# Layer 0 of a four-layer graph network: the keys divided at 1024, masked scores negated, the row minimum carried from part to part

## The chip, the core and the metric

The kernel runs on one core of a Trainium2 chip, in float32 throughout. The core's engines work from queues of their own and wait for one another through semaphores. The names of the profile are used below: PE is TensorE (PEld its weight loads), DVE is VectorE, ACT is ScalarE, POOL is GpSimd, SP is SyncE, which here only issues DMAs. The metric is the device time of one launch in microseconds (us), lower is better.

## The reference, cut to what matters

Four graph layers are applied to 2708 nodes with 512 features; the adjacency matrix `adj` is 2708 x 2708, of zeros and ones, with a full diagonal. Each layer's result is added to its input and layer-normed. The change touches layer 0 alone, masked attention with 8 heads of 64:

```python
def _L0_gnn_ref(node_matrix, adjacency_matrix, Wks, Wqs, Wvs, Wo):
    ...
    adj = jnp.maximum(adjacency_matrix, jnp.eye(n, dtype=adjacency_matrix.dtype))
    keys = jnp.einsum('nj,hjk->hnk', node_matrix, Wks)
    queries = jnp.einsum('nj,hjk->hnk', node_matrix, Wqs)
    values = jnp.einsum('nj,hjk->hnk', node_matrix, Wvs)
    atts = jnp.einsum('hqk,hmk->hqm', queries, keys) / key_dim ** 0.5
    atts = atts - 1e+16 * (1.0 - adj)[None, :, :]
    atts = jax.nn.softmax(atts, axis=-1)
    return jnp.einsum('hqm,hmk,hko->qo', atts, values, Wo)
...
x = _layernorm(x + _L0_gnn_ref(x, adj, ...), axis=-1)
```

Layers 1 and 3 are normalized graph convolutions and layer 2 is a second attention; nothing of them is changed.

## The kernel before, in words

The 2708 nodes are 22 chunks of 128 (`NC = 22`, the last one has 20 rows). Layer 0 first projects keys (`KT`), values (`V`) and queries, then works through 85 items. An item is one chunk of 128 queries and one pair of heads (`Pair(c, p)`, four pairs a chunk); the last chunk, of 20 queries, does its four pairs in one item (`Last`), which goes first.

For each item the 2708 keys are taken in two parts, `k = 0` and `k = 1`, which begin at the chunks in `bounds` (0 and 11: 1408 and 1300 keys). The steps of an item:

- `scores(k, part)`: each part of the keys in three slices (`PARTS = 3`, of 469, 470, 433 or 434 keys). For each slice PE makes the products of the two heads (line 419) into two PSUM banks; DVE adds the mask (0 or -1e16) and keeps the slice's row maximum (line 441, one instruction for each head). A `READ_ACCUMULATOR` instruction behind each of them writes that maximum into a column of `mx`. That is 12 slices by head in an item.
- `maxima()`: DVE takes the largest of the six columns of each head, negated (`nm`, line 454).
- `weights(k)`: ACT computes exp(s - maximum) in place, one instruction for each head, with the row's sum (line 460).
- The weights must be turned, keys on the partitions, before they can be multiplied with the values. The first 8 chunks of each part (`DEALT = 8`) are turned by DVE in 32 x 32 blocks (`blocks(k)`, line 466, into a buffer `d`) and then dealt over the partitions by four DMAs of 256 KB (`deal(k)`, line 475, from `d` into a buffer `e`). The other chunks (`turned`: 8, 9, 10 and 19, 20, 21) are turned on PE (`turn()`, line 492) and copied out of PSUM by ACT (lines 495 to 498).
- `values()`: PE multiplies the turned weights with V (line 511) into the PSUM bank `av`; ACT copies the result (line 529) and POOL's queue stores it (line 530).

The order on PE, DVE and ACT is the program's own (`manual_schedule`). Three items are in work at a time. In iteration i `new` is item i, `cur` item i-1 and `late` item i-2, and each engine does:

- PE: `new.scores`, `late.values`, `cur.turn`
- DVE: `new.scores` (12), `maxima`, `cur.blocks(1)` (both heads in one instruction of 128 x 2048), `new.blocks(0)` (an instruction of 128 x 1024 for each head), and in every fourth iteration `loops` (line 209) between the scores
- ACT: `cur.weights(1)`, a row sum (line 195) and the mask (line 215) of the next chunk in three of four iterations, `new.weights(0)`, the copy of `av`, three copies out of `turn`
- SP: the loads for the next chunk, `cur.deal(1)`, `new.deal(0)`

The buffers: scores `s0` and `s1` (one for each part of the keys, two buffers each), `d` two buffers, `e` three, the PSUM banks of scores and turned blocks (`ps_s`) seven in turn, `av` one. A buffer is written again only when all who used it are done.

Of the kernel before, what the change touches and what calls it, by code (L numbers as in the profile page):

```python
# [8 lines left out]
F32 = mybir.dt.float32  # L9
AF = mybir.ActivationFunctionType  # L10
ALU = mybir.AluOpType
AX = mybir.AxisListType
# [3 lines left out]
P = 128  # L16
BLK = 512
LN_EPS = 1e-5
LOW = -3.0e38
# [3 lines left out]
def kernel(  # L23
# [22 lines left out]
    nc = tc.nc  # L46
# [4 lines left out]
    NC = (N + P - 1) // P  # L51
# [6 lines left out]
    def cols(b):  # L58
        return b * BLK, min(BLK, N - b * BLK)
# [6 lines left out]
    small = ctx.enter_context(tc.tile_pool(name="small", bufs=4))  # L66
# [51 lines left out]
    ends = [0, 8, 16, NC]  # L118
    KD4 = P // 32
    HALVES = 2  # L120
    PARTS = 3
    DEALT = 8
    bounds = [0, NC // 2, NC]

    def dealt(c):
        return any(a <= c < a + DEALT for a in bounds[:-1])
# [19 lines left out]
    with ExitStack() as l0:  # L146
# [19 lines left out]
        def load_chunk(c, k):  # L166

            r0, q = rows(c)
            if k == 0:
                a = adjp.tile([P, N], F32, tag="adj", name=f"adj{c}")  # L170
                qt = io.tile([P, NP, P], F32, tag="qt", name=f"qt{c}")
                loaded[c] = (a, qt)
            a, qt = loaded[c]
            if k < NW:
                n0, w = batch(k)
                if c < LAST:
                    nc.sync.dma_start(a[:q, n0 : n0 + w], adj[r0 : r0 + q, n0 : n0 + w])
                    return

                for g in range(0, P, 32):  # L180
                    nc.sync.dma_start(a[g : g + 32, n0 : n0 + w], adj[N - 32 :, n0 : n0 + w])
            else:
                if c == LAST:
                    nc.sync.dma_start(qt[:, :, :FILL], qtd[c - 1][:, :, P - FILL :])
                nc.sync.dma_start(qt[:, :, FILL:32] if c == LAST else qt, qtd[c])

        def row_sums(c, k):

            r0, q = rows(c)
            a = loaded[c][0]  # L190
            n0, w = batch(k)
            dst = dgp[:, c, k : k + 1]
            if c == LAST:
                q, dst = 32, dgz[:, k : k + 1]
            nc.scalar.activation(a[:q, n0 : n0 + w], a[:q, n0 : n0 + w], AF.Copy, accum_out=dst[:q])
            if c == LAST and k == NW - 1:
                nc.sync.dma_start(dgp[:LR, c, :], dgz[FILL:32, :])

        def loops(c, k):

            r0, q = rows(c)
# [15 lines left out]
        with tc.tile_pool(name="kvw", bufs=1) as kvw, tc.tile_pool(name="xTb", bufs=2) as xtp, tc.tile_pool(  # L217
            name="ps_0", bufs=8, space=PSUM
# [63 lines left out]
            for b in order:  # L282
                n0, w = cols(b)
# [100 lines left out]
        ps_a = l0.enter_context(tc.tile_pool(name="ps_a", bufs=1, space=PSUM, reuse_waits="tile"))  # L384
        ps_s = l0.enter_context(tc.tile_pool(name="ps_s", bufs=7, space=PSUM, reuse_waits="tile"))
        sp = l0.enter_context(tc.tile_pool(name="sp", bufs=2, reuse_waits="tile"))
        dp = l0.enter_context(tc.tile_pool(name="dp", bufs=2, reuse_waits="tile"))
        ep = l0.enter_context(tc.tile_pool(name="ep", bufs=3, reuse_waits="tile"))
        ptp = l0.enter_context(tc.tile_pool(name="ptp", bufs=1, reuse_waits="tile"))

        def half(k):

            n0 = bounds[k] * P
            return n0, min(bounds[k + 1] * P, N) - n0

        def bank(shape, name):
            return ps_s.tile(shape, F32, tag="s", name=name)
# [3 lines left out]
        class Pair:  # L401


            def __init__(self, c, p):
                self.c, self.p = c, p
                self.s = []
                self.mx = small.tile([P, 2, HALVES * PARTS], F32, tag="mx", name=f"mx{c}_{p}")
                self.D = {}
                self.E = {}
                self.pts = {}  # L410
                self.done = 0
                self.av = None
# [15 lines left out]
            def scores(self, k, part):  # L428

                c, p = self.c, self.p  # L430
                a = loaded[c][0]
                n0, w = half(k)
                if part == 0:
                    self.s.append(sp.tile([P, 2, w], F32, tag=f"s{k}", name=f"s{c}_{p}_{k}"))
                s = self.s[k]
                h0, h1 = (w * i // PARTS for i in (part, part + 1))
                col = k * PARTS + part
                pss = [bank([P, BLK], f"pss{c}_{p}_{col}_{j}") for j in range(2)]
                self.products(pss, n0 + h0, h1 - h0)
                for j in range(2):  # L440
                    nc.vector.tensor_tensor_reduce(  # L441
                        out=s[:, j, h0:h1],
                        in0=pss[j][:, : h1 - h0],
                        in1=a[:, n0 + h0 : n0 + h1],
                        scale=1.0,
                        scalar=LOW,
                        op0=ALU.add,
                        op1=ALU.max,
                        accum_out=self.mx[:, j, col : col + 1],
                    )  # L450

            def maxima(self):
                self.nm = small.tile([P, 2], F32, tag="nm", name=f"nm{self.c}_{self.p}")
                nc.vector.tensor_reduce(self.nm, self.mx, AX.X, ALU.max, negate=True)  # L454

            def weights(self, k):

                for j in range(2):
                    s = self.s[k][:, j, :]
                    nc.scalar.activation(s, s, AF.Exp, bias=self.nm[:, j : j + 1], accum_out=self.sums(j, k))  # L460

            def blocks(self, k, heads=slice(0, 2)):

                if k not in self.D:
                    self.D[k] = dp.tile([P, KD4, 2, DEALT, 32], F32, tag="d", name=f"d{self.c}_{self.p}_{k}")
                nc.vector.transpose(  # L466
                    self.D[k].rearrange("p i j m x -> p j m i x")[:, heads],
                    self.s[k][:, heads, : DEALT * P].rearrange("p j (m i x) -> p j m i x", i=KD4, x=32),
                )

            def deal(self, k):
# [139 lines left out]
        with tc.manual_schedule(  # L611
            engines={mybir.EngineType.PE, mybir.EngineType.DVE, mybir.EngineType.Activation}
        ):
            for i in range(len(items) + 2):
                new = None
                more = i < len(items) and items[i][0] < LAST - 1
                prep = more and items[i][1] > 0
                if cur is not None:
                    cur.weights(1)
                if i < len(items):  # L620
                    c, p = items[i]
                    if more:
                        load_chunk(c + 1, p)
                    new = (Pair if c < LAST else Last)(c, p)
                    for part in range(PARTS):
                        new.scores(0, part)
                    if prep:
                        row_sums(c + 1, p - 1)
                    new.scores(1, 0)
                    if prep:  # L630
                        loops(c + 1, p - 1)
                        mask(c + 1, p - 1)
                    for part in range(1, PARTS):
                        new.scores(1, part)
                    new.maxima()
                    new.weights(0)
                if i in (HALF0 * NP + 2, len(items)):
                    sums = heads_sums(i == len(items))
                if late is not None:
                    late.values()  # L640
                if cur is not None:
                    cur.blocks(1)
                    cur.deal(1)
                if new is not None:
                    for j in range(2):
                        new.blocks(0, slice(j, j + 1))
                    new.deal(0)
                if cur is not None:
                    cur.turn()
                if i in (HALF0 * NP + 3, len(items) + 1):  # L650
                    heads_rows(*sums)
                if i == NP:
                    last_sums()
                late, cur = cur, new
# [83 lines left out]
    with tc.tile_pool(name="wo", bufs=1, reuse_waits="tile") as wop:  # L738
        wo_sb = wop.tile([P, KC, D], F32, tag="wo", name="wo_sb")
        load_rows(wo_sb, wo)  # L740
        for c in range(NC):
# [5 lines left out]
            heads = rz_d if c == LAST else rs_d[c >= HALF0][c % HALF0]  # L747
            heads = heads.rearrange("j p q -> j (p q)")
# [129 lines left out]
    if True:  # L878
# [115 lines left out]
        for b in range(NB):  # L994
            for m, _ in enumerate(graph1(b)):
# [90 lines left out]
    if True:  # L1086
# [84 lines left out]
    with tc.tile_pool(name="zp", bufs=2) as zp:  # L1171
# [87 lines left out]
        w = cols(TAIL)[1]  # L1259
# [129 lines left out]
```

## Time and profile before

| what | before |
|---|---|
| median of 3 runs (lowest to highest) | 2587.2 us (2579.19 to 2588.0) |
| the profiled execution | 2581.24 us, of which the span from the first to the last instruction is 2579.4 us |
| mean granted TensorE clock | 0.993 |
| busy in the span: PE, DVE, ACT, POOL | 2508.7, 1962.2, 1154.0, 315.7 us |
| layer 0's 85 items (span 211 to 1226 us): PE, DVE, ACT busy, DMA share | 1003.8, 969.8, 745.5 us of 1015 us, 0.77 |
| before them (0 to 211 us): DVE busy | 117.2 us |
| after them (1226 to 2579 us): DVE busy | 875.2 us |

In the timeline a line gives the start and the length of an instruction in us, the engine, the line of the kernel, the operation, output and inputs with their shapes (partitions x elements), and in brackets how long the engine stood idle before it and what ended that. Consecutive instructions of one line are merged (x3). Instructions of DVE overlap a little: the next one can start some 0.08 us before the length of the last one is over, so the distance from start to start is what an instruction costs in a queue that is never empty.

### The profile page before, as it was taken

To read this page: it belongs to the slowest core of one execution; us is meant where nothing else is said; L and a number is where in the kernel's file an instruction comes from. 1 tells how busy PE (TensorE), PEld (TensorE's weight loads), DVE (VectorE), ACT (ScalarE), POOL (GpSimd) and SP (SyncE) were. 2 spreads that over 40 slices of the span, in tenths; PEclk is the share of its full clock that TensorE was granted. 3 is DMA by queue.
4 is the path that set the end of the run, shared out by engine and by line. 5 is a ranking of instruction groups with operands and counts; after the bars stand their busy time and mean duration, and the time that the engine had idled before them with its cause. 6 is when DMAs were issued, how large, how long until landed. Compare 5 with 4: busy or idle time off the path is not lost. (4 is left out here: it accounts for less than half of the span.)

```text
span 2579.4 us, 42415 instructions
## 1 busy us (share of the span) xinstructions
PE 2508.7 (97%) x15551; PEld 1558.2 (60%) x15551; DVE 1962.2 (76%) x4541; ACT 1154.0 (45%) x2070; POOL 315.7 (12%) x322
## 2 busy tenths in 40 slices
PE   9998999999999999999899999899999999999997
PEld 4886777777777777777456444444444465444465
DVE  3668999999999999999574777988776874543544
ACT  3104778777777777776011001565665640000000
POOL 2110000000000000000210000243332430000000
PEclk9999999999999999999999999999999999999999
DMA  5114787877877777877853444354433213644633
GB/s 167 62 50 138 218 226 211 240 213 220 230 210 219 218 211 215 225 204 186 236 169 94 126 121 142 118 158 138 125 109 116 64 31 114 184 141 143 178 103 105
DMA packets 221498, 411.43 MB, mean 160 GB/s; under 512 B 28765, under 2 KB 48911, under 8 KB 221292
## 3 DMA queue, kind: packets, MB, share of 16 engines
q1 hardware_dynamic: 215052, 392.00, 53.4%
q0 software_dynamic: 6240, 16.73, 1.9%
q8 instruction: 123, 2.02, 0.3%
q14 instruction: 83, 0.68, 0.1%
HBM read 213.55 MB, written 16.72 MB: 89 GB/s over the span
## 5 line engine op out<-in xcount | busy, mean ns | idle before, releaser
L460 ACT ACTIVATE s<-s,nm 128x1408 f32<-128x1408 f32 (+1 forms) x340 | 481.1, 1416 | 244.3 <-DVE nm L454 244.3
L441 DVE CUSTOM_DVE_ANT_0 s<-pss,adj 128x469 f32<-128x469 f32 (+2 forms) x1020 | 565.8, 622 | 8.2 <-PE pss L419 7.0
L419 PE MATMUL pss<-KT,qt 64*128 64x469 f32 (+2 forms) x2016 | 463.7, 561 | 7.2 <-DVE mx L441 4.6
L466 DVE STREAM_TRANSPOSE d<-s 128x1024 f32<-128x1024 f32 (+1 forms) x255 | 393.7, 1580 | 31.6 <-DMA e<-d 16.1
L419 PEld LDWEIGHTS pss<-KT,qt 64*128 64x128 f32 x2016 | 230.1, 187 | 200.3 <-issue 110.8
L811 PE MATMUL acc<-pt,x 128*128 128x512 f32 (+1 forms) x880 | 333.4, 537 | 12.2 <-ACT pt L864 9.7
L511 PE MATMUL av<-e,V 128*64 128x128 f32 x5376 | 309.6, 273 | 4.7 <-DMA e<-d 4.7
L511 PEld LDWEIGHTS av<-e,V 128*64 128x64 f32 x5376 | 297.8, 137 | 5.1 <-issue 5.1
L811 PEld LDWEIGHTS acc<-pt,x 128*128 128x128 f32 x880 | 157.2, 191 | 188.1 <-issue 162.2
L917 PE MATMUL acc<-at,h 128*128 128x512 f32 (+1 forms) x504 | 196.8, 543 | 0.0
L875 POOL TENSOR_TENSOR cs<-cs,pt 128x512 f32<-128x512 f32 (+2 forms) x110 | 157.3, 1430 | 202.7 <-ACT pt L864 200.4
L862 DVE TENSOR_TENSOR pt<-pt,at 128x512 f32<-128x512 f32 (+2 forms) x132 | 107.3, 820 | 75.6 <-ACT pt L861 75.4
L530 POOL DMA_DIRECT2D otd<-ot x84 | 45.2, 538 | 941.7 <-ACT ot L529 921.4
L94 ACT ACTIVATE ln_t<-lnve 128x1 f32<-128x1 f32 x88 | 17.7, 201 | 313.2 <-DVE lnve L108 313.1
L1251 ACT ACTIVATE z<-pz,rdeg 128x512 f32<-128x512 f32 (+1 forms) x22 | 15.1, 688 | 310.9 <-PE pz L823 310.9
L917 PEld LDWEIGHTS acc<-at,h 128*128 128x128 f32 x504 | 90.2, 190 | 101.4 <-issue 99.2
L492 PE MATMUL pst<-ident,s 128*128 128x128 f32 x1020 | 130.0, 277 | 0.0
L864 ACT ACTIVATE pt<-pt 128x512 f32<-128x512 f32 (+2 forms) x132 | 76.1, 579 | 110.0 <-DVE pt L863 109.8
L511 PEld LDWEIGHTS av<-pt,V 128*64 128x64 f32 x1680 | 90.0, 136 | 52.3 <-issue 51.5
L928 DVE SCALAR_TENSOR_TENSOR cs<-at,rdeg,cs 128x512 f32<-128x512 f32 (+2 forms) x126 | 86.2, 684 | 43.7 <-DMA at<-in_adjT_dram 42.4
L492 PEld LDWEIGHTS pst<-ident,s 128*128 128x128 f32 x1020 | 104.2, 133 | 16.8 <-issue 15.1
L511 PE MATMUL av<-pt,V 128*64 128x128 f32 x1680 | 110.3, 278 | 0.2 <-ACT pt L498 0.2
(348 smaller groups left out, 3474.5 us busy)
## 6 DMA issues: line engine op xcount, KB each, us to landing
e<-d SPq DMA_DIRECT2D x680, 256.0 KB
at<-in_adjT_dram SPq DMA_DIRECT2D x210, 256.0 KB
a<-in_adj_dram SPq DMA_DIRECT2D x38, 677.0 KB
adj<-in_adj_dram SPq DMA_DIRECT2D x42, 512.0 KB
at_a<-in_adjT_dram SPq DMA_DIRECT2D x40, 256.0 KB
at_c<-in_adjT_dram SPq DMA_DIRECT2D x40, 256.0 KB
at_f<-in_adjT_dram SPq DMA_DIRECT2D x40, 256.0 KB
adj<-in_adj_dram SPq DMA_DIRECT2D x21, 330.0 KB
```

Of the source, the lines that this page charges most:

```text
L419: nc.tensor.matmul(pss[j][:, :w], qt[h, self.p, :], KT[h, self.p, n0 : n0 + w], start=True, stop=True)
L441: nc.vector.tensor_tensor_reduce(out=s[:, j, h0:h1], in0=pss[j][:, : h1 - h0], in1=a[:, n0 + h0 : n0 + h1], scale=1.0, scalar=LOW, op0=ALU ...
L460: nc.scalar.activation(s, s, AF.Exp, bias=self.nm[:, j : j + 1], accum_out=self.sums(j, k))
L466: nc.vector.transpose(self.D[k].rearrange("p i j m x -> p j m i x")[:, heads], self.s[k][:, heads, : DEALT * P].rearrange("p j (m i x) -> ...
L492: nc.tensor.transpose(pt[:q, t, j, :], self.s[f][:, j, o : o + q], ident)
L511: nc.tensor.matmul(self.av[j * KD : (j + 1) * KD, out], V[:, m, h * KD : (h + 1) * KD], weights[j], start=(self.done == 0), stop=(self.don ...
L811: nc.tensor.matmul(acc[k][:, :w], last[0][g : g + mr, :] if m == NC - 1 else values[:mr, k * P : (k + 1) * P], moving[g : g + mr, :w], sta ...
L862: nc.vector.tensor_tensor(pt[:mr, :w], pt[:mr, :w], at[:mr, :w], ALU.subtract)
L864: nc.scalar.activation(pt[:mr, :w], pt[:mr, :w], AF.Exp)
L875: nc.gpsimd.tensor_tensor(sums[:mr, :w], sums[:mr, :w], pt[:mr, :w], ALU.add)
L917: nc.tensor.matmul(acc[hc][:, :w], lastH[g : g + mr, :] if m == NC - 1 else H[m][:mr, hc * P : (hc + 1) * P], at[g : g + mr, :w], start=(m ...
L928: nc.vector.scalar_tensor_tensor(sums[:mr, :w], at[:mr, :w], rdeg[:mr, m : m + 1], sums[:mr, :w], ALU.mult, ALU.add)
```

## The change

The second part of the keys now begins at chunk 8 (`bounds = [0, 8, 22]`): the parts have 1024 and 1684 keys, in 2 and 4 slices (512 and 421 keys). Chunks 0 to 7 and 8 to 15 are dealt, 16 to 21 are turned on PE, all of them from the second part. The scores are stored negated (`scale=-1.0`), so that the row's extreme is a minimum; each slice starts its minimum from the column that the slice in front of it wrote (`scalar=self.mx[:, j, col - 1 : col]`, a value for each partition, read from memory; the first slice of each head has the constant `-LOW`). The last column is then the minimum of all keys, and `maxima()` is gone; exp is taken with `scale=-1.0` and that column as its bias. `s0` has one buffer instead of two, `d` three instead of two, and `new.blocks(0)` turns both heads in one instruction.

```diff
-    PARTS = 3
+    PARTS = (2, 4)
     DEALT = 8
-    bounds = [0, NC // 2, NC]
+    bounds = [0, DEALT, NC]
...
-        dp = l0.enter_context(tc.tile_pool(name="dp", bufs=2, reuse_waits="tile"))
+        dp = l0.enter_context(tc.tile_pool(name="dp", bufs=3, reuse_waits="tile"))
...
-                    self.s.append(sp.tile([P, 2, w], F32, tag=f"s{k}", name=f"s{c}_{p}_{k}"))
+                    self.s.append(sp.tile([P, 2, w], F32, tag=f"s{k}", name=f"s{c}_{p}_{k}", bufs=k + 1))
...
-                h0, h1 = (w * i // PARTS for i in (part, part + 1))
-                col = k * PARTS + part
+                h0, h1 = (w * i // PARTS[k] for i in (part, part + 1))
+                col = sum(PARTS[:k]) + part
...
                     nc.vector.tensor_tensor_reduce(
                         out=s[:, j, h0:h1],
                         in0=pss[j][:, : h1 - h0],
                         in1=a[:, n0 + h0 : n0 + h1],
-                        scale=1.0,
-                        scalar=LOW,
+                        scale=-1.0,
+                        scalar=self.mx[:, j, col - 1 : col] if col else -LOW,
                         op0=ALU.add,
-                        op1=ALU.max,
+                        op1=ALU.min,
                         accum_out=self.mx[:, j, col : col + 1],
                     )
-            def maxima(self):
-                self.nm = small.tile([P, 2], F32, tag="nm", name=f"nm{self.c}_{self.p}")
-                nc.vector.tensor_reduce(self.nm, self.mx, AX.X, ALU.max, negate=True)
...
-                    nc.scalar.activation(s, s, AF.Exp, bias=self.nm[:, j : j + 1], accum_out=self.sums(j, k))
+                    nc.scalar.activation(s, s, AF.Exp, scale=-1.0, bias=self.mx[:, j, -1:], accum_out=self.sums(j, k))
...
-            def blocks(self, k, heads=slice(0, 2)):
-                if k not in self.D:
-                    self.D[k] = dp.tile([P, KD4, 2, DEALT, 32], F32, tag="d", name=f"d{self.c}_{self.p}_{k}")
+            def blocks(self, k):
+                self.D[k] = dp.tile([P, KD4, 2, DEALT, 32], F32, tag="d", name=f"d{self.c}_{self.p}_{k}")
                 nc.vector.transpose(
-                    self.D[k].rearrange("p i j m x -> p j m i x")[:, heads],
-                    self.s[k][:, heads, : DEALT * P].rearrange("p j (m i x) -> p j m i x", i=KD4, x=32),
+                    self.D[k].rearrange("p i j m x -> p j m i x"),
+                    self.s[k][:, :, : DEALT * P].rearrange("p j (m i x) -> p j m i x", i=KD4, x=32),
                 )
...
-                    new.maxima()
                     new.weights(0)
...
-                    for j in range(2):
-                        new.blocks(0, slice(j, j + 1))
+                    new.blocks(0)
                     new.deal(0)
```

More of the change, by code (lines that the diff above doesn't have):

```diff
@@ L406, in __init__ @@
                 self.s = []
-                self.mx = small.tile([P, 2, HALVES * PARTS], F32, tag="mx", name=f"mx{c}_{p}")
+                self.mx = small.tile([P, 2, sum(PARTS)], F32, tag="mx", name=f"mx{c}_{p}")
                 self.D = {}
@@ L624 @@
                     new = (Pair if c < LAST else Last)(c, p)
-                    for part in range(PARTS):
+                    for part in range(PARTS[0]):
                         new.scores(0, part)
@@ L632 @@
                         mask(c + 1, p - 1)
-                    for part in range(1, PARTS):
+                    for part in range(1, PARTS[1]):
                         new.scores(1, part)
-                    new.maxima()
                     new.weights(0)
```

## The prediction

> **What bounds the kernel now.** The change touches only layer 0's 85 items, so I read the groups of instructions first for those lines, then one iteration in the timelines of DVE and PE, then DVE's waits over 300 to 1200 us.
>
> From the page (groups; last columns: busy us, mean ns, idle before and its releaser):
>
> ```profile
> L460 ACT ACTIVATE s<-s,nm 128x1408 f32<-128x1408 f32 (+1 forms) x340 | 481.1, 1416 | 244.3 <-DVE nm L454 244.3
> L441 DVE CUSTOM_DVE_ANT_0 s<-pss,adj 128x469 f32<-128x469 f32 (+2 forms) x1020 | 565.8, 622 | 8.2 <-PE pss L419 7.0
> L466 DVE STREAM_TRANSPOSE d<-s 128x1024 f32<-128x1024 f32 (+1 forms) x255 | 393.7, 1580 | 31.6 <-DMA e<-d 16.1
> ```
>
> ACT has 244 us to spare. DVE hardly waits before its scores, and 31.6 us before its transposes. One undisturbed iteration, DVE from `nm` to `nm`, then PE from turn to turn:
>
> ```profile
> 256.55 0.17 DVE L454 TENSOR_REDUCE nm<-mx 128x2 f32<-128x12 f32 x1
> 256.75 4.56 DVE L466 STREAM_TRANSPOSE d<-s 128x2048 f32<-128x2048 f32 x3
> 261.25 0.65 DVE L441 CUSTOM_DVE_ANT_0 s<-pss,adj 128x469 f32<-128x469 f32 x1
> ...
> 267.83 0.09 DVE L441 DVE_READ_ACCUMULATOR2_ANT mx<- 128x1 f32 x1
> 267.95 0.17 DVE L454 TENSOR_REDUCE nm<-mx 128x2 f32<-128x12 f32 x1
> ...
> 258.70 1.53 PE L492 MATMUL pst<-ident,s 128*128 128x128 f32 x12
> ...
> 260.16 5.06 PE L419 MATMUL pss<-KT,qt 64*128 64x469 f32 x24
> ...
> 265.15 1.31 PE L511 MATMUL av<-pt,V 128*64 128x128 f32 x20
> ...
> 270.10 1.53 PE L492 MATMUL pst<-ident,s 128*128 128x128 f32 x12
> ```
>
> DVE: 0.20 from `nm` to the transposes, 4.50 for three transposes, 6.58 for twelve slices, 0.12 from the last read of the accumulator to `nm`: 11.40 us, with no idle in it. PE: 1.46 turning, 4.99 scores, 4.95 values: also 11.40, dense. So both engines have the same floor. Yet from 281.26 to 1216.59 us there are 79 iterations in 935.3 us, 11.84 each. The 37 of them with no idle on DVE in front of a transpose have a mean of 11.47 (11.41 without, about 11.60 with a `loops` instruction, which takes 0.2); the other 42 have 12.17. The waits behind that:
>
> ```profile
> DVE d L466 <- DMA e<-d: 15.1, 30, 1.5
> DVE d L466 <- ACT ot L529: 5.5, 6, 1.0
> DVE d L466 <- ACT pt L498: 3.3, 2, 1.9
> ```
>
> Nothing that `blocks` reads comes from `ot` or `pt`, so those waits too are the DMA's. With two `d` buffers `blocks(0)` writes what the dealing of the last `blocks(0)` has to have left, 11.40 - 2.3 = 9.1 us later; only that transpose waits, hardly ever `blocks(1)`.
>
> **The change part by part**, on DVE, which has no slack.
>
> 1. Third `d` buffer. `blocks(0)` now takes the buffer that `blocks(1)` left a whole iteration (over 11 us) earlier, and those DMAs are issued first of the eight; `blocks(1)` waits on DMAs twice as old. Before, `blocks(1)` came 9.5 us after the `blocks(1)` whose buffer it took and did not wait, so landing within 9.5 us is shown and the waits end. Worth 42 x (12.17 - 11.47) = 29 us at most (12.17 also holds some `loops`), 26 us by the idle alone. PE's use of `e` is two iterations behind for part 0 and PE waited for no DMA in this stretch, so the DMA has nowhere new to be late.
>
> 2. `nm` gone: 0.12 + 0.20 = 0.32 us an item. The transposes read no `mx`, so the first can follow the last slice directly.
>
> 3. One transpose for both heads: the three took 4.50 start to start. The 128x1024 form takes 1.13 start to start (1.067 for its elements if one takes 1/0.96 ns, which is what 469 against 433 elements, 0.567 against 0.53 us, gives), so the 128x2048 form 4.50 - 2.26 = 2.24; two are 4.48: 0.02 saved, 0.1 if the large one's fixed part is as small as the other's. I take 0.06. It must wait for both heads' exp. A 1408-wide exp takes 1.47 start to start, a 1300-wide 1.38, so a 1024-wide one 1.15. The first head's minimum is ready one slice (0.57) before the last; exp then ends about 1.9 us after the last slice, under `blocks(1)`'s 2.24. If waits went by the whole `mx` tile it would end at some 2.5, a stall of 0.3 or 24 us over the run. ACT itself is free: `weights(1)` grows by 2 x 0.32 (1684 for 1300 keys) and `weights(0)` may come 0.8 earlier, against an idle of 244.3/85 = 2.9 us an item.
>
> 4. The carried minimum: ten of an item's twelve slices now read a scalar from memory. No slice of before does. The nearest rows, instructions of 512 elements a partition, first without such a scalar, then with one (`rc`, `rdeg`):
>
> ```profile
> 102.65 0.69 DVE L236 TENSOR_TENSOR cx<-xp 128x512 f32<-128x512 f32 x1
> 103.25 0.69 DVE L237 TENSOR_TENSOR cx<-xp 128x512 f32<-128x512 f32 x1
> ...
> 1429.44 0.29 DVE L945 TENSOR_TENSOR rc<-pcs,rdeg 128x1 f32<-128x1 f32 x3 [0.63 <-PE pcs L734]
> 1429.65 0.74 DVE L952 SCALAR_TENSOR_TENSOR y<-b_sb,rc,x 128x512 f32<-128x512 f32 x1
> 1430.31 0.75 DVE L928 SCALAR_TENSOR_TENSOR cs<-at,rdeg,cs 128x512 f32<-128x512 f32 x1
> 1430.97 0.15 DVE L945 TENSOR_TENSOR rc<-pcs,rdeg 128x1 f32<-128x1 f32 x1
> ```
>
> 0.60 start to start without, 0.66 with: 0.06 for the scalar. Bounds: 0, if the accumulator read between two slices covers the fetch, and 0.12, what `nm` lost waiting for the read just ahead of it. I take 0.06, the row nearest in kind: 10 x 0.06 = 0.60 us an item. The order of reads is harmless: a slice's scalar was written by the read two slices back, with the other head's slice between, and L952 above, which reads column 0 of `rc`, started 0.07 behind the write of column 2, so waits go by column. Negating, the constant of the first slice and exp's scale are constants in place of constants: 0. The elements (2 x 2708) and the number of slices stay, so 6.58 + 0.60.
>
> 5. One `s0` buffer: the first slice overwrites what the transpose right ahead of it reads. The nearest pair is L381 writing what the reduction L382 ahead of it read:
>
> ```profile
> 187.25 0.69 DVE L382 TENSOR_REDUCE u<-wk_sb 128x1 f32<-128x512 f32 x1
> 187.97 0.69 DVE L381 TENSOR_TENSOR wk_sb<-wk_sb 128x512 f32<-128x512 f32 x1
> ```
>
> 0.72, where independent ones take 0.60: 0.12. I take that; 0 is the other end. PE no longer reads `s0`, so nothing but DVE and ACT's finished exp stands in front of it.
>
> 6. PE: 512 and 421 keys for 469 and 433 are the same columns, matmuls and turned blocks; 0. It falls from co-bound to 0.3 us of slack, and cannot go below 11.40.
>
> **The sum.** An iteration of DVE: 6.58 + 0.60 + 4.44 + 0.12 = 11.74; `loops` in every fourth adds 0.05: 11.79, against 11.84. Over 79 iterations that is 4 us less; what was won from the DMA (29) goes back into ten slower slices (47) less `nm` and the merged transpose (30) and plus the overwritten buffer (9). From the profiled execution's 2581.2 that makes 2577; the median of the runs shown is 6 higher, which would make it 2583. I name 2579. My forecast is no change. Its own range: the overwrite at 0 gives 13 less, the scalar at 0.07 gives 8 more: 2566 to 2590.
>
> [...]
>
> **The rivals.**
>
> *The scalar is free (0.22).* Then DVE needs 11.74 - 0.60 = 11.14 and PE becomes the bound at 11.41: 79 x 0.43 = 34 us less, 2547. For it: the accumulator read already costs next to nothing beside the slice that follows. Against: every row with a scalar shows its 0.06, also back to back.
>
> *The carried column is waited for (0.16), slower.* Place: each of the ten slices on DVE, which has no slack. Price: 0.12 instead of 0.06, 0.60 more an item: 12.39, 79 x 0.55 = 43 us more, 2624. It decides from 0.07 a slice on, where the iteration passes 11.84, and is past my bound of 13 us at 0.08. For it: the read right ahead of `nm` did cost 0.12. Against: here it lies one slice back.
>
> *The third buffer does not end the waits (0.08),* because the dealing itself is behind, not the buffer: then 26/79 = 0.33 stays in each iteration, 12.12, 22 us more: 2603. For it: the DMA share is already 0.77. Against: undisturbed stretches run at 11.40 with the same DMAs, and `blocks(1)` never waits.
>
> **How the numbers follow.** No change 0.50, of which 0.10 lies lower than 0.5% (13 us, about what a measurement of this kernel can tell); the rivals 0.22, 0.16, 0.08; 0.04 is left to stalls I do not see, half of them slower ones. Faster: 0.22 + 0.10 + 0.01 = 0.33. Slower: of 0.16 some 0.14, of 0.08 all but 0.02, 0.02 of the rest and 0.02 of the forecast: 0.24. Same: 0.43. The range runs from the free scalar, 2545, to just short of the full price of the wait, 2618.
>
> **What would show it.** Step 4: slices of 512 and 421 start 0.67 and 0.57 apart (0.61 and 0.52 if free, 0.73 and 0.63 if waited for). Step 1: no idle of DVE before L466. Step 2: the first transpose starts with the last accumulator read. Step 3: none of the idle before L466 is ACT's exp. Step 5: 0.12 more from the last transpose to the first slice. Step 6: PE's iteration has gaps before L419 that end with DVE. What would make it wrong most easily is step 4, whose error counts 790 times.

## The result, and the profile after

| | before | after |
|---|---|---|
| median (lowest to highest) of 6 runs each | 2586.46 us (2578.86 to 2588.0) | 2603.6 us (2598.36 to 2608.85) |
| ratio to before, 95% interval | 1 | 1.0075 [1.0057, 1.0093] |
| profiled execution, its span | 2581.24, 2579.4 us | 2603.68, 2601.9 us |
| mean granted TensorE clock | 0.993 | 0.989 |

The changed kernel is 0.75% slower: the means of the six runs are 19 us apart, the spans of the two profiled executions, which are compared below, 22.5 us. The time lies inside the predicted range, but the forecast, no change, was wrong: a gain of 4 us was expected.

From the page of the changed kernel, the groups that answer to those of before (the slices are now two groups, with and without `mx` as a scalar):

```profile
L456 ACT ACTIVATE s<-s,mx 128x1024 f32<-128x1024 f32 (+1 forms) x340 | 480.9, 1415 | 224.5 <-DVE mx L441 224.4
L441 DVE CUSTOM_DVE_ANT_0 s<-pss,adj,mx 128x421 f32<-128x421 f32 (+1 forms) x850 | 514.6, 671 | 0.0
...
L461 DVE STREAM_TRANSPOSE d<-s 128x2048 f32<-128x2048 f32 x170 | 382.4, 2286 | 1.9 <-ACT s L456 1.9
...
L441 DVE CUSTOM_DVE_ANT_0 s<-pss,adj 128x512 f32<-128x512 f32 x170 | 110.7, 689 | 31.1 <-PE pss L419 18.3
```

The transposes stood idle 31.6 us before and 1.9 us now, none of it for a DMA. The slices are busy 625.3 us instead of 565.8. Of these idle times only one has grown, that in front of the slices: 31.1 us against 8.2, all before the first slice of a head. Of these, 16.4 belong to the third iteration below; most of the rest are 0.14 us in nearly every item. One steady iteration of DVE, from transpose to transpose:

```profile
606.73 0.08 DVE L441 DVE_READ_ACCUMULATOR2_ANT mx<- 128x1 f32 x1
606.73 4.50 DVE L461 STREAM_TRANSPOSE d<-s 128x2048 f32<-128x2048 f32 x2
611.37 0.69 DVE L441 CUSTOM_DVE_ANT_0 s<-pss,adj 128x512 f32<-128x512 f32 x1
...
612.60 0.74 DVE L441 CUSTOM_DVE_ANT_0 s<-pss,adj,mx 128x512 f32<-128x512 f32 x1
...
613.27 0.74 DVE L441 CUSTOM_DVE_ANT_0 s<-pss,adj,mx 128x512 f32<-128x512 f32 x1
...
613.94 0.65 DVE L441 CUSTOM_DVE_ANT_0 s<-pss,adj,mx 128x421 f32<-128x421 f32 x1
...
614.52 0.65 DVE L441 CUSTOM_DVE_ANT_0 s<-pss,adj,mx 128x421 f32<-128x421 f32 x1
...
618.56 4.50 DVE L461 STREAM_TRANSPOSE d<-s 128x2048 f32<-128x2048 f32 x2
```

The second of the two merged transposes alone, from a window that begins behind the first:

```profile
608.96 2.27 DVE L461 STREAM_TRANSPOSE d<-s 128x2048 f32<-128x2048 f32 x1
```

Read the distances of the starts: 0.67 for a 512-wide slice with the carried column, 0.58 for a 421-wide one, 7.19 for all twelve (611.37 to 618.56), 4.64 from the first transpose to the first slice. Together 11.83. The second transpose starts 2.23 behind the first (606.73 to 608.96), and the slice 2.41 behind the second. In an experiment below the slice behind the second transpose writes another buffer and starts 2.20 behind it. So the two transposes by themselves take 4.43 of the 4.64, and 0.21 are left.

To find the 22.5 us I took the start of the first slice of each item from both traces and subtracted iteration by iteration:

| stretch | before, us | after, us | difference |
|---|---|---|---|
| start of the first slice of all | 210.0 | 211.2 | +1.2 |
| iterations 1 and 2 | 11.16 + 11.23 | 11.59 + 11.83 | +1.0 |
| iteration 3 | 17.44 | 28.27 | +10.8 |
| iterations 4 and 5 | 11.40 + 13.31 | 11.83 + 13.34 | +0.5 |
| the 79 behind them | 79 x 11.84 | 79 x 11.963 | +9.7 |
| from the last item's first slice to the end | 1369.5 | 1368.8 | -0.7 |

So there are two losses of about the same size: a single iteration, the third, and a small sum in each of the 79.

**The third iteration.** It holds `values()` of the last chunk, with its four pairs of heads and 20 columns for each matmul. PE, before:

```profile
240.20 2.03 PE L511 MATMUL avz<-e,V 128*64 128x20 f32 x64
```

PE after, and the first slice of DVE that stands behind it:

```profile
244.62 1.24 PE L506 MATMUL avz<-pt,V 128*64 128x20 f32 x20
...
245.90 3.59 PE L506 MATMUL avz<-e,V 128*64 128x20 f32 x64
```

```profile
262.92 0.69 DVE L441 CUSTOM_DVE_ANT_0 s<-pss,adj 128x512 f32<-128x512 f32 x1 [16.38 <-PE pss L419]
```

The same 64 matmuls take 3.59 us instead of 2.03. The table by windows of 5 us (PE, its weight loads, DVE, ACT and POOL busy, with counts, then the granted clock, the DMA share and GB/s) says why, first before, then after:

```profile
240.00:245.00 5.00, 5.00 (x180) 5.00 (x176) 4.13 (x3) 2.77 (x7) 0.00 (x0) 1.00 0.10 36
```

```profile
240.00:245.00 5.00, 5.00 (x96) 5.00 (x98) 5.00 (x10) 2.53 (x5) 0.00 (x0) 0.50 0.37 117
245.00:250.00 5.00, 5.00 (x100) 5.00 (x98) 1.53 (x1) 0.19 (x2) 0.00 (x0) 0.50 0.00 0
250.00:255.00 5.00, 5.00 (x100) 5.00 (x98) 0.00 (x0) 0.17 (x1) 0.00 (x0) 0.50 0.02 3
```

PE is busy all the time in both, but after the change its clock is granted at 0.50, from 234.7 to 262 us, so a window holds 100 matmuls instead of 180. DVE and ACT have nothing to do meanwhile: PE's products for the next item are queued behind these matmuls.

### The profile page after: what moved, and what is told of

Same layout as the page of the kernel before. It is cut to its first block, busy times and chain, and to the rows that moved or that the text cites. A ratio compares the mean times of both kernels' runs of the same rounds, so it can differ in the third digit from the quotient of the medians.

```text
span 2601.9 us, 43200 instructions
## 1 busy us (share of the span) xinstructions
PE 2532.1 (97%) x15551; PEld 1560.5 (60%) x15551; DVE 1988.6 (76%) x4371; ACT 1170.5 (45%) x2070; POOL 316.2 (12%) x322
## 3 DMA queue, kind: packets, MB, share of 16 engines
q8 instruction: 124, 2.03, 0.3%
## 4 chain that ended last, share of the span: by engine, by line
issue 49%; PE 41%; DVE 4%; POOL 2%; DMA 2%; ACT 1%; SPq 1%; POOLq 0%; ACTq 0%; DVEq 0%
PE acc L804 12%; PE acc L910 7%; PE m L1214 5%; PE pf L816 2%; PE po L750 2%; PE psk L261 2%; POOL otd L525 2%; PE ph L896 1%; PE psv L261 1%; PE psq L261 1%; PE p L941 1%; PE pz L816 1%; PE psv L357 1%; PE acc_t L804 1%; PE psq L309 1%
## 5 line engine op out<-in xcount | busy, mean ns | idle before, releaser
L456 ACT ACTIVATE s<-s,mx 128x1024 f32<-128x1024 f32 (+1 forms) x340 | 480.9, 1415 | 224.5 <-DVE mx L441 224.4
L441 DVE CUSTOM_DVE_ANT_0 s<-pss,adj,mx 128x421 f32<-128x421 f32 (+1 forms) x850 | 514.6, 671 | 0.0
L419 PE MATMUL pss<-KT,qt 64*128 64x421 f32 (+1 forms) x2016 | 477.2, 565 | 6.2 <-DVE mx L441 5.2
L461 DVE STREAM_TRANSPOSE d<-s 128x2048 f32<-128x2048 f32 x170 | 382.4, 2286 | 1.9 <-ACT s L456 1.9
L419 PEld LDWEIGHTS pss<-KT,qt 64*128 64x128 f32 x2016 | 223.5, 187 | 220.8 <-issue 140.1
L441 DVE CUSTOM_DVE_ANT_0 s<-pss,adj 128x512 f32<-128x512 f32 x170 | 110.7, 689 | 31.1 <-PE pss L419 18.3
L487 PEld LDWEIGHTS pst<-ident,s 128*128 128x128 f32 x1020 | 105.3, 134 | 16.9 <-issue 8.3
```

The costliest lines, as they stand in the source:

```text
L419: nc.tensor.matmul(pss[j][:, :w], qt[h, self.p, :], KT[h, self.p, n0 : n0 + w], start=True, stop=True)
L441: nc.vector.tensor_tensor_reduce(out=s[:, j, h0:h1], in0=pss[j][:, : h1 - h0], in1=a[:, n0 + h0 : n0 + h1], scale=-1.0, scalar=self.mx[:, ...
L456: nc.scalar.activation(s, s, AF.Exp, scale=-1.0, bias=self.mx[:, j, -1:], accum_out=self.sums(j, k))
L461: nc.vector.transpose(self.D[k].rearrange("p i j m x -> p j m i x"), self.s[k][:, :, : DEALT * P].rearrange("p j (m i x) -> p j m i x", i= ...
L487: nc.tensor.transpose(pt[:q, t, j, :], self.s[f][:, j, o : o + q], ident)
```

## The experiments

The theory I took into them: the two halves are separate. The steady half is the single `s0` buffer (4.64 from the first transpose to the first slice) and the ten scalars; the other half is the clock in the third iteration. The rivals: that the third `d` buffer brings nothing; that what `s0` seems to cost is something else behind the transposes; that PE is slow in the third iteration for want of data and not of clock. Edits are against the changed kernel unless another is named. Ratios are to the kernel before on the same chip; "steady" is the mean of the 79 iterations, "floor" their shortest usual length.

### The third buffer taken away

```diff
-tc.tile_pool(name="dp", bufs=3, reuse_waits="tile")
+tc.tile_pool(name="dp", bufs=2, reuse_waits="tile")
```

> The changed kernel with two d buffers instead of three; all else as changed. Theory (the third buffer ends the DMA waits of DVE): the waits before the transposes come back. From before's 79 iterations, 31 of which took longer than 11.83 us, 16 us in all above it: 12 to 20 us more than the changed kernel, about 2617 us, with 10 to 20 us of DVE idle before L461 put down to DMA. Rival (in the changed kernel DVE is slow enough that the dealing is always done in time, so the third buffer does nothing there): within 3 us of the changed kernel, no such idle.

Measured: 2620.34 us (2618.55 to 2624.83), ratio 1.0153 [1.0134, 1.0171]; steady 12.144, floor 11.83 as in the changed kernel. The waits of DVE between 300 and 1200 us (what waited for what: us in all, times, longest) show the removed wait again:

```profile
DVE d L461 <- DMA e<-d: 10.9, 19, 1.2
```

The third buffer is worth (12.144 - 11.963) x 79 = 14 us at this pace. The profiled execution is 14.9 us longer than that of the changed kernel. The third iteration took only 17.63 in it, with the small matmuls at full clock, 10.6 less; but the part from the last item's first slice on, nearly all of it unchanged code, took 1379.3 instead of 1368.8. Of that it lost 4.6 us between 1258 and 1369 us, where the mean clock was 0.94 against 0.97 in the same work of the changed kernel, and 5.5 us between 1651 and 1778 us, at 0.92 against 0.96. So the clock differs between executions also where no edit is; whether the one loss has to do with the other is not shown.

### Two `d` and two `s0` buffers

```diff
-... tag=f"s{k}", name=f"s{c}_{p}_{k}", bufs=k + 1))
+... tag=f"s{k}", name=f"s{c}_{p}_{k}"))
```

beside the edit above. One `d` buffer and one `s0` buffer are each 128 x 2048 float32, 8 KB a partition, so the first gives up what the second takes.

> As e1 (two d buffers), and s0 with two buffers again, so that the first slice of an item doesn't overwrite what the transpose right ahead of it reads. Theory (in the changed kernel 0.26 us between the last transpose and the first slice are the wait of that overwrite: 4.64 us from the first transpose to the first slice, where two transposes at 2.19 make 4.38): undisturbed iterations fall from 11.83 to 11.57 us; since DMA waits then take a part of it back, 8 to 18 us less than e1. Rival (the 0.26 us belong to the two long transposes or to their four DMA semaphores): from the first transpose to the first slice still 4.64, same time as e1 within 3 us.

Measured: 2608.17 us (2600.56 to 2616.75), ratio 1.0110 [1.0076, 1.0145]; steady 12.044, floor 11.73, first transpose to first slice 4.58.

```profile
619.20 4.50 DVE L461 STREAM_TRANSPOSE d<-s 128x2048 f32<-128x2048 f32 x2
623.78 0.69 DVE L441 CUSTOM_DVE_ANT_0 s<-pss,adj 128x512 f32<-128x512 f32 x1
```

A second `s0` buffer brought the floor down by 0.10, less than I had expected. Of the 45 steady iterations with no wait between the two transposes, 14 take 4.42 to the slice, which is the transposes' own time. In 28 others DVE stands idle 0.04 to 0.08 us in front of the slice, probably for PE's product, which the slice reads; what ended so short an idle is not shown. Three `d` with two `s0` buffers, which would take 8 KB more a partition, was not tried, nor was the kernel before with a third `d` buffer alone.

### The reduction in place of the carried minimum

```diff
-                        scale=-1.0,
-                        scalar=self.mx[:, j, col - 1 : col] if col else -LOW,
+                        scale=1.0,
+                        scalar=LOW,
                         op0=ALU.add,
-                        op1=ALU.min,
+                        op1=ALU.max,
...
+                    new.maxima()
                     new.weights(0)
```

with `maxima()` and the bias `nm` of the kernel before; `d`, `s0` and the merged transpose stay as changed.

> The changed kernel with the maximum as before: no column is read by a slice, scores are not negated, a reduction over the six columns makes nm before exp; the division at 1024, three d and one s0 buffer stay. Theory (ten slices cost 0.06 us more each for the scalar that they read, 0.60 an item, against 0.32 for the reduction and the gap ahead of it): undisturbed iterations 11.83 - 0.60 + 0.32 = 11.55 us, 79 x 0.28 = 22 us less than the changed kernel, about 2582; slices of 512 and 421 start 0.61 and 0.52 apart. Rival (the slices of 512 and 421 are slower in themselves): they stay at 0.67 and 0.58, and the time rises by the reduction's 79 x 0.3 = 25 us to about 2628. The four products of the last chunk's values, which ran at a granted clock of 0.50 from 235 to 261 us in the changed kernel and cost 10.8 us there: if the cause is how long PE idled just before, the shorter slices leave PE less idle and the clock may come back to 1.0 (another 10 us less, 2572); if it belongs to the new order of work, it stays.

Measured: 2600.81 us (2595.36 to 2602.66), ratio 1.0071 [1.0052, 1.0090]; steady 11.947. That is (11.963 - 11.947) x 79 = 1 us, where 22 were expected. A miss, and the most instructive one. DVE, with the second transpose also by itself:

```profile
616.11 0.59 DVE L441 CUSTOM_DVE_ANT_0 s<-pss,adj 128x421 f32<-128x421 f32 x1
616.62 0.08 DVE L441 DVE_READ_ACCUMULATOR2_ANT mx<- 128x1 f32 x1
616.74 0.17 DVE L454 TENSOR_REDUCE nm<-mx 128x2 f32<-128x12 f32 x1
616.95 4.71 DVE L465 STREAM_TRANSPOSE d<-s 128x2048 f32<-128x2048 f32 x2
...
619.35 2.31 DVE L465 STREAM_TRANSPOSE d<-s 128x2048 f32<-128x2048 f32 x1
621.80 0.69 DVE L441 CUSTOM_DVE_ANT_0 s<-pss,adj 128x512 f32<-128x512 f32 x1
```

ACT, at the same time:

```profile
616.94 1.15 ACT L460 ACTIVATE s<-s,nm 128x1024 f32<-128x1024 f32 x1 [2.77 <-DVE nm L454]
...
618.09 1.13 ACT L460 ACTIVATE s<-s,nm 128x1024 f32<-128x1024 f32 x1
619.13 0.19 ACT L460 ACTIVATION_READ_ACCUMULATOR s<-s,nm 128x1 f32 x1
```

And ACT in the changed kernel:

```profile
606.27 1.15 ACT L456 ACTIVATE s<-s,mx 128x1024 f32<-128x1024 f32 x1 [1.73 <-DVE mx L441]
```

The slices did fall to 0.61 and 0.52 start to start, 0.60 less an item. Then 0.33 goes to the reduction (616.62 to 616.95). The rest is in the exp: `nm` releases both heads' exps at once, at 616.94. The read of the second one's row sum ends at 619.32. The second transpose, which turns both heads, has to wait for it: it starts at 619.35, 2.40 behind the first instead of 2.23. So from transpose to slice it is 4.85 instead of 4.64, 0.21 more, of which this wait is 0.17, and 0.33 + 0.21 = 0.54 of the 0.60 is given back. With the carried column the first head's exp starts a slice early, 0.46 us before DVE's transposes (606.27 against 606.73), and the wait does not arise. In this kernel, with one transpose for both heads, the carried minimum costs what it saves.

### The other part of the keys first

```diff
+                    new.scores(1, 0)
                     for part in range(PARTS[0]):
                         new.scores(0, part)
...
-                    new.scores(1, 0)
```

The first slice behind the transposes is then one of `s1`, which has two buffers; the carried column follows the new order (a running number in place of `col`).

> The changed kernel with the first slice of the second part of the keys taken before the two slices of the first part (the columns of the minimum are carried in that order). Nothing else moves; three d and one s0 buffer. The slice that overwrites s0 now has two slices between itself and the transpose that reads s0. Theory (overwrite wait): from the first transpose to the first slice 4.38 instead of 4.64 us, undisturbed iterations 11.57, 79 x 0.26 = 20 us less than the changed kernel, about 2583. Rival (the 0.26 us belong to the transposes): 4.64 and 2603 as in the changed kernel.

Measured: 2578.75 us (2573.6 to 2589.22, 10 runs), ratio 0.9982 [0.9967, 0.9997]; steady 11.767, floor 11.58. DVE, with the second transpose also by itself:

```profile
611.19 4.49 DVE L463 STREAM_TRANSPOSE d<-s 128x2048 f32<-128x2048 f32 x2
...
613.42 2.26 DVE L463 STREAM_TRANSPOSE d<-s 128x2048 f32<-128x2048 f32 x1
615.62 0.55 DVE L443 CUSTOM_DVE_ANT_0 s<-pss,adj 128x421 f32<-128x421 f32 x1
```

The distance is 4.43 here instead of 4.64, and the floor falls by 0.25. The overwrite of `s0` right behind its transpose is the cause: with two `s0` buffers 4.42 was there too, in 14 of 45 iterations. It needs no second buffer but only another slice in between. That slice has 421 columns, not 512, so PE's first product is also a shorter one; what that adds was not tried apart. The third iteration took 17.1 us, at full clock. Both halves together, (11.963 - 11.767) x 79 = 15 and 11 us, are about the 24 us between the ratios 1.0075 and 0.9982.

### Work for PE ahead of the small matmuls

```diff
             def values(self):
+                warm = ps_a.tile([P, BLK], F32, tag="av", name="warm")
+                for _ in range(5):
+                    nc.tensor.matmul(warm, ident, KT[:, 0, :BLK], start=True, stop=True)
                 self.avs = [
```

in `Last` alone: five matmuls of 512 columns whose product nobody reads.

> The changed kernel with five matmuls of 128 x 512 in front of the values of the last chunk (iteration 2), their result unused, written into the bank of av that is free then; nothing else is changed. Theory (the 28.3 us of that iteration, against 17.4 before, come from the granted clock: PE waits at 231 to 240 us, the clock falls to 0.50 and the 20-column matmuls of the values never bring it back, so that 352 of them run at half speed): the five long matmuls, about 4 us at half clock, bring the clock back to 1.0, the values run at some 2.6 us a pair as before, and the iteration takes 28.3 - 10 + 4 = 21 to 23 us; 5 to 8 us less than the changed kernel, about 2597. Rival (the values are slow because of what they read or wait for, or the clock is held down whatever PE does there): the clock stays at 0.50, the iteration takes 32 us, 4 us more, about 2608.

Measured: 2601.6 us (2597.81 to 2605.15, 10 runs), ratio 1.0062 [1.0046, 1.0078]; steady 11.964, third iteration 24.84. PE:

```profile
238.94 6.92 PE L556 MATMUL warm<-KT,ident 128*128 128x512 f32 x10
245.79 0.77 PE L506 MATMUL avz<-pt,V 128*64 128x20 f32 x20
...
246.51 2.03 PE L506 MATMUL avz<-e,V 128*64 128x20 f32 x64
248.38 0.74 PE L506 MATMUL avz<-pt,V 128*64 128x20 f32 x20
```

The pair that took 4.70 us now takes 2.59 (245.79 to 248.38), on the same data in the same places. Without the 6.92 us of extra work the iteration would be 17.9, near the 17.44 of before. So the clock is the cause of the long iteration, not a late transfer. As a remedy it is worth little: it gives 3.4 us in the iteration, where 5 to 8 were expected, and the intervals of the two ratios overlap.

### Reduction, transposes by head, other part first

The kernel of "the other part of the keys first", with the reduction back and the transpose of part 0 by head:

```diff
-                    new.blocks(0)
+                    for j in range(2):
+                        new.blocks(0, slice(j, j + 1))
```

> e4 (second part's first slice first) with the reduction of e3 in place of the carried minimum, and blocks(0) for each head by itself as before, so that its first transpose doesn't wait for the second head's exp. Three d buffers, one s0. Theory (step 4 of the change costs 10 x 0.06 and pays back 0.33 of the reduction and, since exp starts earlier, the 0.2 us that e3 shows DVE waiting between its two transposes; with a transpose for each head that wait is gone too, and then PE is the bound): DVE 6.58 + 0.33 + 2.19 + 2.26 = 11.36, PE 11.40; iterations of 11.40 to 11.45 where nothing disturbs, a mean of 11.5 to 11.6 against 11.77 of e4: 13 to 20 us less than e4, about 2562. Rival (the wait for exp stays, since the second head's exp ends 2.4 us after nm and the first transpose of blocks(0) can only start then; or the dealing is late again at this pace): 11.6 and more, within 8 us of e4.

Measured: 2569.17 us (2564.67 to 2570.94), ratio 0.9932 [0.9909, 0.9954]; steady 11.617, floor 11.36. The third iteration took 22.14, with the clock at 0.50 from 244.2 to 254.5 us. In the steady stretch one wait is left that matters:

```profile
DVE adj L209 <- ACT adj L195: 9.5, 16, 0.7
```

`loops` now stands behind 6 of the 12 slices and reads the row sum that ACT makes behind `weights(1)`, which has grown. In the changed kernel the same wait is already there, 3.0 us in 12 places:

```profile
602.75 0.08 DVE L441 DVE_READ_ACCUMULATOR2_ANT mx<- 128x1 f32 x1
603.06 0.29 DVE L209 TENSOR_TENSOR adj<-adj,ident 128x128 f32<-128x128 f32 x1 [0.23 <-ACT adj L195]
```

### `loops` two slices later

The kernel above, with one more slice of each head ahead of `loops`, as in the kernel before, where it stood behind 8:

```diff
+                    new.scores(1, 1)
                     if prep:
                         loops(c + 1, p - 1)
                         mask(c + 1, p - 1)
-                    for part in range(1, PARTS[1]):
+                    for part in range(2, PARTS[1]):
```

> e6 with the instruction that sets the mask's diagonal (loops, L209 of before) moved behind one more slice of each head on DVE (after 8 of 12 as before the change, not after 6). Theory (the longer exp of the second part, 2 x 1.69 us for 2 x 1.37, makes ACT's row sum late, and DVE waits 0.2 to 0.4 us for it ahead of loops in one of four iterations, then takes 0.2 for it: 12.3 against 11.6 in e4): those iterations lose the wait, about 0.35 us each in some 14 of them: 3 to 6 us less than e6. Rival (the wait goes to exp of the first part instead, since the mask then stands later in ACT's order): no difference, or 2 us more.

Measured: 2555.61 us (2548.53 to 2556.54), ratio 0.9872 [0.9831, 0.9913], the best of all: 1.3% faster than the kernel before. Steady 11.489, floor 11.36, third iteration 16.95. DVE, and its waits from 300 to 1180 us:

```profile
601.76 4.57 DVE L468 STREAM_TRANSPOSE d<-s 128x2048 f32<-128x2048 f32 x3
606.70 0.60 DVE L443 CUSTOM_DVE_ANT_0 s<-pss,adj 128x421 f32<-128x421 f32 x1 [0.38 <-PE pss L420]
```

```profile
DVE s L443 <- PE pss L420: 2.7, 5, 0.8
...
DVE d L468 <- DMA e<-d: 0.4, 1, 0.4
```

The wait for `loops` is gone. DVE's own work is the floor (6.87 from the first slice to the first transpose, 4.49 from there to the next slice); it stands before PE's products only five times. PE's busy time does not tell how near PE is to a floor of its own, for it is as full at either pace: 877.6 of these 880 us here, and 899.8 of the 900 us from 300 to 1200 in the changed kernel, whose iterations are 0.47 us longer. More was gained than the 9.5 us of that wait: (11.617 - 11.489) x 79 = 10 us, and 5 us from the clock in the third iteration.

### The carried minimum in the best order

The kernel of "the other part of the keys first" with `loops` two slices later: the best kernel, but with carried minimum and merged transpose.

> e4 (carried minimum, second part's first slice first, three d, one s0, one transpose for both heads) with loops behind one more slice of each head, as in e7; so e7 with the carried minimum and the merged transpose in place of the reduction and a transpose for each head. Theory (what the carried minimum costs by itself where nothing else holds DVE back: ten slices at 0.06 against 0.33 for the reduction and 0.07 for the third transpose; DVE 11.58, above PE's 11.36 to 11.40): iterations of 11.58, with loops 11.8; mean 11.63 to 11.68, 79 x 0.16 = 11 to 15 us more than e7 in the iterations, about 2568. Rival (the carried minimum is worth as much as it costs, since it lets exp start earlier): within 4 us of e7, about 2555.

Measured: 2569.65 us (2563.84 to 2573.81), ratio 0.9951 [0.9931, 0.9971]; steady 11.678, floor 11.58, third iteration 16.9. Against the best kernel that is 0.19 x 79 = 15 us, 14 us between the medians and 20 between the ratios. Here the scalars cost more than the reduction, because with transposes by head the first of them no longer waits for both exps: 0.60 against 0.33 for the reduction and 0.07 for the third transpose.

### The best kernel with two `d` buffers

The edit of the first experiment, on the best kernel.

> e7 with two d buffers instead of three. Theory (at the pace of 11.4 us the dealing is late in half the iterations, as before the change, where it was priced at 26 to 29 us): DVE waits for DMA ahead of its transposes again, 20 to 28 us in all, the mean iteration goes from 11.49 to about 11.8: 20 to 28 us more than e7, about 2580. Rival (e1's price holds at this pace too, since DVE and PE share the lost time): 12 to 17 us more, about 2570.

Measured: 2583.24 us (2573.82 to 2590.51, 10 runs), ratio 1.0009 [0.9992, 1.0026]; steady 11.819, floor 11.36.

```profile
DVE d L468 <- DMA e<-d: 18.1, 25, 1.3
```

The third buffer is worth (11.819 - 11.489) x 79 = 26 us here, against 14 at the slower pace: at the faster pace the dealing has not left the buffer in 25 iterations instead of 19, and the waits are 18.1 us instead of 10.9. In this profile the third iteration also lost some clock (22.31).

## Why the prediction was wrong

By its own steps:

- **Step 1, third buffer, 26 to 29 us:** right. The DMA waits are gone (31.6 to 1.9 us idle, none of it for a DMA). Taken alone, it is worth 14 us at 11.83 an iteration and 26 at 11.36, near the pace at which the prediction had counted it. The rival that it ends no waits fell; that its price, 2603 us, is close to the time measured is chance.
- **Step 2, `nm` gone, 0.32:** right. The first transpose starts with the last accumulator read, both at 606.73.
- **Step 3, one transpose, 4.44 for two:** right, 4.43. The stall on the exp was not there (1.9 us in the whole run). The prediction weighed this stall only for late columns; the reduction makes it (0.2 us an item), and the carried column is what avoids it.
- **Step 4, 0.06 a slice:** right. 7.19 against the 7.18 of the sum, 0.67 and 0.58 apart. That the scalar would be free or waited for, the two largest rivals, both fell.
- **Step 5, one `s0` buffer, 0.12:** too small. 4.64 - 4.43 = 0.21, and with another slice in between it goes. The row from which the 0.12 came is an operation of 512 elements behind another; behind a transpose of 2048 the wait was nearly twice as long. 0.09 x 79 = 7 us.
- **`loops`, 0.05 on the mean:** what lies above the floor is 0.13 (11.963 against 11.83), 0.08 x 79 = 6.5 us more. Some 4 us of that are the wait in front of `loops`: 12 of its iterations took 12.34 to 12.40, the 6 without the wait 12.03. Its place behind the slices moved from 8 to 6, and the exp in front of its row sum became longer. The prediction saw that `weights(1)` grows, and took it for covered since ACT is free. It is free, but DVE waits for this one row sum. The other 2.5 us are three iterations that the sum left out (13.44, 12.75 and 12.18 us; the same three took 13.28, 12.15 and 11.75 before).
- **Step 6, PE 0:** right in the steady stretch, not in the third iteration. The gaps before L419 that it named as a sign are not there (0.2 us in one place from 300 to 1200 us), and 11.40 was not the least: iterations of 11.36 were seen.
- **The range of the forecast:** by its own terms an overwrite at 0 takes off 9 us, not 13, and a scalar of 0.07 adds 8, so 2579 would give 2570 to 2587. The time measured lies outside of this range.

**The step that failed most** is one that the sum made without saying: it went over 79 iterations and took everything around them as unchanged. There the kernel lost 13 of the 22.5 us, 10.8 in the third iteration, where the clock was granted at 0.50 while the last chunk's small matmuls ran. That this is the clock is shown by the extra matmuls ahead of them. The other part is the steady sum: 9.7 us more instead of 4 less. Those 13.7 us are 7 (step 5) and 6.5 (`loops` and the three iterations). The time is inside the wide range by luck: it was laid out for two rivals of step 4, and neither came true.

The traces show when the clock fell and came back (windows of 1 us put it to the tenth), but not in full why. The changed kernel, then the one with two `d` buffers, which lost nothing in the third iteration:

```profile
234.00:235.00 1.00, 0.47 (x2) 0.00 (x0) 0.86 (x2) 1.00 (x2) 0.00 (x0) 0.84 0.86 170
261.00:262.00 1.00, 1.00 (x5) 0.58 (x5) 0.00 (x0) 0.73 (x3) 0.00 (x0) 0.50 0.94 189
262.00:263.00 1.00, 1.00 (x6) 0.44 (x6) 0.09 (x1) 1.00 (x3) 0.00 (x0) 1.00 0.88 217
```

```profile
235.00:236.00 1.00, 0.23 (x1) 0.23 (x2) 0.99 (x3) 1.00 (x3) 0.00 (x0) 0.77 1.01 260
238.00:239.00 1.00, 1.00 (x6) 0.82 (x4) 1.00 (x6) 0.23 (x2) 0.00 (x0) 0.53 0.92 195
239.00:240.00 1.00, 1.00 (x15) 0.39 (x15) 1.00 (x4) 0.94 (x1) 0.00 (x0) 1.00 0.98 272
```

| kernel | clock at 0.50, us | small matmuls, us | third iteration |
|---|---|---|---|
| before | 232.6 to 236.0 | 236.9 to 247.4 | 17.4 |
| changed, two `d` | 235.5 to 238.9 | 239.6 to 250.1 | 17.6 |
| changed, extra matmuls | 236.9 to 243.7 | 245.8 to 256.2 | 24.8 |
| changed | 234.7 to 262.0 | 239.9 to 258.9 | 28.3 |
| reduction | 234.2 to 261.5 | 239.7 to 258.7 | 28.1 |
| reduction, transposes by head, other part first | 244.2 to 254.5 | 236.2 to 250.0 | 22.1 |
| best, two `d` | 245.0 to 255.3 | 236.7 to 250.6 | 22.3 |

So the clock fell before the change too, behind a gap of PE. What decided in these traces is whether it was back when the small matmuls began: where it was not, or where it fell among them, it came back only 2.8 to 4.7 us behind their end. In the remaining kernels it was at 1.00 when they began and stayed there. Why it was back after 3.4 us in some and not in the changed kernel stays open: with two `d` buffers the gaps of PE in front were nearly the same (0.87 and 0.93 us, against 1.05 and 0.94). It is not a chance of the one execution alone: in all six runs of the changed kernel the mean clock was 0.986 to 0.989, in 39 of the 43 runs of the kernel before that stood beside the experiments 0.990 or more, and 27 us at half clock are 0.005 of that mean. Where in the run the clock was lost, only the profiled execution tells.

The spells of the table last 3.4, 6.8, 10.3 or 27.3 us, close to one, two, three or eight times 3.4. The idle stretches of PE just ahead of these falls were of 0.6 to 2.3 us, and in the changed kernel PE was busy throughout from 240 to 255 us, at 0.50, without the clock coming back. What sets the length of a spell is not shown.

## What to carry to other kernels

Sum the first and the last iterations of a pipeline on their own: here a single iteration at a lower clock cost 10.8 us, more than the 9.7 of the 79 steady ones. When two edits of a change are priced apart, look for the wait that one of them covers: the carried minimum alone costs 0.60 an item, but it starts an exp early that the merged transpose needs. And where a buffer is overwritten right behind its last reader on the same engine, put an instruction of another buffer in between before paying for a second buffer: here that alone brought 4.64 us down to 4.43.

## What the runs showed of the hardware

- A value for each partition as the scalar adds 0.06 us to a slice on DVE, back to back, at 421 and at 512 elements: 0.52 to 0.58 and 0.61 to 0.67.
- A DVE instruction that writes what the transpose directly ahead of it reads started 2.41 us behind the start of that transpose; one that writes another buffer started 2.20 behind it: the wait cost 0.21.
- PE busy without a gap on matmuls of 20 columns stayed at a granted clock of 0.50 for 15 us and more where the clock was low when they began (239.9 to 258.9 us in the changed kernel); where it was at 1.00, it could stay there through all 352 of them (236.9 to 247.4 us before the change). With five matmuls of 512 columns ahead of them (6.92 us from 238.94) it was at 1.00 from 243.7 us on.
- The clock of the whole run hardly shows such a loss (0.989 against 0.993, for some 11 us in one iteration); windows of 5 us do.
